# Two graph attention layers as one fixed-order pipeline over groups of edges, in a graph network on one core

## The chip, the core and the metric

The kernel runs on one core of a Trainium2 chip. A core has TensorE (PE in the profile; its weight loads are shown as PEld), VectorE (DVE), ScalarE (ACT), GpSimd (POOL) and SyncE (SP), which issues most transfers. The metric is the device time of one execution in microseconds, lower is better. All data are float32.

## The reference

A graph has 3125 nodes with 256 channels and 53125 edges, sorted by their destination node; each edge has 32 attributes and one of three types. Two attention layers run over the edges, then three relational layers:

```python
def transformer_conv(x, ...):             # 4 heads of 64 channels
    q, k, v = x @ wq + bq, x @ wk + bk, x @ wv + bv
    alpha = sum(q[dst] * k[src], -1) / sqrt(64)          # per edge and head
    ex = exp(alpha - segment_max(alpha, dst)[dst])
    alpha = ex / segment_sum(ex, dst)[dst]
    return segment_sum(v[src] * alpha, dst) + x @ ws + bs
h = leaky_relu(batch_norm(transformer_conv(x, layer 1)))
h = leaky_relu(batch_norm(transformer_conv(h, layer 2)))
x = layernorm(x + h)
# three times: message = relu(x[src] * (edge_attr @ nn_w.T + nn_b)),
# the mean of the messages per destination and type, @ W[type], summed, + x @ root + bias
out = layernorm(x + relational(x))
```

Batch norm goes over the nodes for each channel, layer norm over the channels of each node.

## The kernel before

The nodes lie in 25 blocks of 128, the edges in 416 tiles of 128 (the last ones padded); eight tiles make a group (G), and there are 52 groups (NG). A partition holds one node between the layers (tiles `xf` and `hf`, 128 x 25 x 256).

`gnn_kernel` builds tables of indices from `src`, `dst` and the types (L146 to L251): the source of each edge for the gathers, the position of its destination in a window of 32 nodes, a penalty where two neighbouring edges have different destinations, the first node of each pair of tiles. Shifted copies of the destinations go through a table in DRAM (`dp`). A flag says whether the edges have the expected form; the program branches on it to `sorted_edges` (L264), which is what runs here.

`window_attention` (L325) is called once for each layer. It has three stages.

1. The projection, for each block of 128 nodes: two transposes (L352), ScalarE's copy (L354), four matmuls of 128x512 for queries, skip, keys and values (L358), VectorE's adds of the biases (L362 to L369). Queries are stored to the table `qw_tab`, keys and values to `kvw_tab` with 4 x 65 columns for the values, whose 65th is 1.0 and later gives the denominator.
2. The loop over groups. `logits(g)`: GpSimd gathers eight times 128 rows of `kvw_tab` by source (L272, tile `kvg`, 4 buffers). SyncE loads the positions (`ldb`, L394), reads four row numbers into registers and loads four windows of 32 query rows (`qw`, L400). VectorE makes one-hot matrices (`oht`, L402), PE expands the queries to the edges with 32-row matmuls (`qdf`, L407), VectorE multiplies with the keys (`prod`, L409) and reduces per head (L411). `sums(g-1)`: SyncE loads the penalties (`pn`, L416); PE turns the logits (L420), VectorE finds the largest logit of each destination by a scan forward and one backward (L423, L425), PE turns it back (L428), VectorE subtracts (L431), ScalarE takes exp (L432). VectorE makes a one-hot over 32 nodes (L434) and multiplies it with the weights, for four heads, twice 128x512 (L438). PE sums weights times values in 32 matmuls with 32 columns of weights and 65 of values (L447), and VectorE adds the results into the accumulator (`accf`, L453, eight instructions with a column offset from registers). In layer 1 `attributes(g)` also turns the edge attributes for the later relational layers: a load of 1 KB per partition (L463), eight transposes (L468), two copies by ScalarE (L469), a store of whole rows to `at_d` (L470).
3. After the loop: a division by the denominators (L484 to L486), 16 transfers that bring the sums back to nodes on partitions (`naf`, L491), an add to the skip (L493), and `batch_norm` (L507 to L528), which sums over nodes with a matrix of ones on PE and applies the result on VectorE.

Behind layer 2 come the residual add (L300), `layer_norm` (L1252 to L1258), the store of `h_tab` (L303), the memset of the relational accumulator (`kacc`, L309) and `window_relational` (L563 to L660), which gathers rows of `h_tab` in the same groups of eight.

In the attention stages the order of instructions on each engine comes from the framework's scheduler, by the program's order and by buffers; only `window_relational` has an order written out by hand. SyncE issues its transfers one after another in its own order, and waits ahead of each for what that one reads.

Of the kernel before, what the change touches and what calls it, by code (L numbers as in the profile page):

```python
# [8 lines left out]
F32 = mybir.dt.float32  # L9
# [9 lines left out]
P = 128  # L19
# [33 lines left out]
W2 = 32  # L53
KN = 42
# [6 lines left out]
def last_group(i, rows):  # L61

    return min(NG - 1, int((E / N * rows * (i + 1) / P + SLACK) // G))

# [38 lines left out]
def gnn_kernel(ctx: ExitStack, tc: tile.TileContext, A, out):  # L103


    nc = tc.nc
# [5 lines left out]
    dp = dram.tile([FP + EP + 2 * P], F32, name="dp")  # L112
    pen_d = dram.tile([FP + EP + 2 * P], F32, name="pen_rows")
    ld_d = dram.tile([EP], F32, name="ld_rows")

    ident = const.tile([P, P], F32, name="identf")
    make_identity(nc, ident)
    src_c = const.tile([P, T], I32, name="src_c")
    lm_c = const.tile([P, T], F32, name="lm_c")
    kr_c = const.tile([P, T], F32, name="kr_c")  # L120
    a_off = const.tile([1, PR], I32, name="a_off")
    q_row = const.tile([1, PR], I32, name="q_row")
    k_off = const.tile([1, Q4], I32, name="k_off")
    a_low = const.tile([P, PR], F32, name="a_low")
    a_high = const.tile([P, PR], F32, name="a_high")
    k_low = const.tile([P, Q4], F32, name="k_low")
    k_high = const.tile([P, Q4], F32, name="k_high")
    flag = const.tile([1, 1], I32, name="flag")

    with tc.tile_pool(name="lk", bufs=1) as sp, tc.tile_pool(name="lkps", bufs=2, space=PSUM) as ps:  # L130
        rows = {}
        for name in ("dst", "src", "edge_type_3"):
# [4 lines left out]
            else:  # L137
# [7 lines left out]
        d = sp.tile([RB, B, P], F32, name="d_f")  # L145
        V.tensor_copy(d, rows["dst"])  # L146
        SY.dma_start(dp[FP:FP + EP].rearrange("(b r c) -> r b c", b=B, c=P), d)
        edge = sp.tile([1, FP + 2 * P], F32, name="edge")
        V.memset(edge[:, :FP], -1.0)
        GP.iota(edge[:, FP:].rearrange("o (a c) -> o a c", c=32), pattern=[[1, 8], [0, 32]], base=N + 4,  # L150
                channel_multiplier=0, allow_small_or_imprecise_dtypes=True)
        SY.dma_start(dp[:FP].unsqueeze(0), edge[:, :FP])
        SY.dma_start(dp[FP + EP:].unsqueeze(0), edge[:, FP:])

        prv = sp.tile([RB, B, P], F32, name="prv")
        nxt = sp.tile([RB, B, P], F32, name="nxt")
        SY.dma_start(prv, dp[FP - 1:FP - 1 + EP].rearrange("(b r c) -> r b c", b=B, c=P))
        SY.dma_start(nxt, dp[2 * FP:2 * FP + EP].rearrange("(b r c) -> r b c", b=B, c=P))
        n0 = sp.tile([RB, B], F32, name="n0")
        n4 = sp.tile([RB, B], F32, name="n4")  # L160
        for b in range(B):
            SY.dma_start(n0[:, b:b + 1], view(dp, FP + b * RB * P, [[2 * P, RB // 2], [0, 2], [1, 1]]))
            SY.dma_start(n4[:, b:b + 1], view(dp, FP + b * RB * P, [[4 * P, RB // 4], [0, 4], [1, 1]]))
        n0r = sp.tile([1, PR], F32, name="n0r")
        n4r = sp.tile([1, Q4], F32, name="n4r")
        SY.dma_start(n0r, view(dp, FP, [[0, 1], [2 * P, PR]]))
        SY.dma_start(n4r, view(dp, FP, [[0, 1], [4 * P, Q4]]))


        pen = sp.tile([RB, B, P], F32, name="pen")  # L170
        V.tensor_tensor(pen, d, prv, op=OP.is_equal)
        V.tensor_scalar(pen, pen, -1.0, BIG, op0=OP.add, op1=OP.mult)
        SY.dma_start(pen_d[FP:FP + EP].rearrange("(b r c) -> r b c", b=B, c=P), pen)
# [5 lines left out]

        ld = sp.tile([RB, B, P], F32, name="ld")  # L180
        V.tensor_tensor(ld, d, bc(n0, 2, P), op=OP.subtract)
        SY.dma_start(ld_d.rearrange("(b r c) -> r b c", b=B, c=P), ld)
        dq = d.rearrange("r b c -> r (b c)")
        _, dm = floor42(V, sp, dq, [RB, B * P], "d42")
# [5 lines left out]
        bad = sp.tile([RB, B, P], F32, name="bad")  # L190
        v = sp.tile([RB, B, P], F32, name="v")
        need = sp.tile([1, NG - 1], F32, name="need")
        V.memset(need, 0.0)
        for i in range(NT):
            V.memset(need[:, last_group(i, KM):], float((i + 1) * KM)) if last_group(i, KM) < NG - 1 else None
        V.tensor_tensor(need, need, n4r[:, 2::2], op=OP.subtract)
        late = sp.tile([1, 1], F32, name="late")
        V.tensor_reduce(late, need, AX.X, OP.max)
        V.tensor_tensor(bad, prv, d, op=OP.subtract)
        V.tensor_tensor(v, d, nxt, op=OP.subtract)  # L200
        V.scalar_tensor_tensor(bad, v, 1.0, bad, op0=OP.add, op1=OP.max)
        V.scalar_tensor_tensor(bad, ld, -float(W2 - 1), bad, op0=OP.add, op1=OP.max)
        V.tensor_tensor(v, d, bc(n4, 2, P), op=OP.subtract)
        V.scalar_tensor_tensor(bad, v, -float(KN - 1), bad, op0=OP.add, op1=OP.max)
        worst = sp.tile([RB, 1], F32, name="worst")
        V.tensor_reduce(worst, bad.rearrange("r b c -> r (b c)"), AX.X, OP.max)
        wt = ps.tile([1, RB], F32, name="wt")
        TE.transpose(wt, worst, ident[:RB, :RB])
        w1 = sp.tile([1, 1], F32, name="w1")
        V.tensor_reduce(w1, wt, AX.X, OP.max)  # L210
        V.tensor_tensor(w1, w1, late, op=OP.max)
        V.tensor_single_scalar(flag, w1, 0.0, op=OP.is_le)


# [5 lines left out]
        for col, v in ((src_c, s_f), (lm_c, lm), (kr_c, kr)):  # L220
            t = ps.tile([P, T], F32, name="colf")
            for b in range(B):
                TE.transpose(t[:, b * RB:(b + 1) * RB], v[:, b, :], ident[:RB, :RB])
# [1144 lines left out]
```

## Time and profile before

| what | value |
|---|---|
| median of 11 runs | 3477.54 us (3460.57 to 3483.32) |
| the profiled execution: time | 3480.43 us |
| its span, first to last instruction | 3478.6 us |
| mean granted clock of TensorE | 0.750 of full speed |
| busy PE / VectorE / ScalarE / GpSimd | 2591.2 / 2238.2 / 625.0 / 2129.8 us |
| first gather of layer 1, of layer 2, of the relational stage | 158.4, 1015.1, 1705.5 us from the start |

The profile is a page on one execution: busy time per engine, the span in 40 slices of 87 us with a digit in tenths for each engine, the chain of work that ended last, and groups of instructions by line, engine and tile, with their mean duration and what ended the idle time before them. The trace behind it also gives a timeline of single instructions and the busy times in any stretch. In a row such as `kvg<-kvw_tab,src_c` the tile written stands left of the arrow. PE, DVE, ACT, POOL and SP are the engines above; "issue" is time in which an engine waited for nothing that the profile shows; the granted clock is the share of full speed that the throttle gave TensorE.

### The profile page before, as it was taken

The page shows a single profiled execution, that of the slowest core. Times are in us where ns is not written, and L with a number is a line of the kernel's source. Part 1 is how long each engine was busy: PE and PEld are TensorE (multiplying, and loading weights), DVE is VectorE, ACT ScalarE, POOL GpSimd, SP SyncE. Part 2 cuts the span into 40 slices and gives each one's busy share as a digit, 9 for nine tenths or more (in the row PEclk, how much of TensorE's full clock was granted, in tenths as well). Part 3 has the DMA queues.
Part 4 walks back from the last instruction along what each step waited for, and adds up shares of the span by engine and source line. Part 5 has one row for each costly group of instructions (what it writes and reads, how often), then busy time and mean ns, then how long its engine had stood idle before and what let it go on. Part 6 is the DMA issues. An engine that isn't in the chain of part 4 may idle for free.

```text
span 3478.6 us, 49513 instructions
## 1 busy us (share of the span) xinstructions
PE 2591.2 (74%) x16663; PEld 1748.9 (50%) x16663; DVE 2238.2 (64%) x4344; ACT 625.0 (18%) x1060; POOL 2129.8 (61%) x2146
## 2 busy tenths in 40 slices
PE   4877777772886777773188888868888886888887
PEld 2444444542444444442166565646556654666665
DVE  4476767895548988894866665545555554666664
ACT  0122222000100000001022222212222221222222
POOL 0165655771027777760377777757777766777774
PEclk9955555555985555556599999978999988998888
DMA  4386766774148888873344444334343433444442
GB/s 125 125 238 198 218 202 197 228 228 109 49 141 234 232 229 232 233 207 70 117 119 116 120 116 118 109 96 116 115 116 113 116 97 101 122 119 122 120 127 77
DMA packets 296342, 510.28 MB, mean 147 GB/s; under 512 B 78243, under 2 KB 194833, under 8 KB 296081
## 3 DMA queue, kind: packets, MB, share of 16 engines
q0 software_dynamic: 126464, 383.52, 38.5%
q1 hardware_dynamic: 169617, 123.51, 11.9%
q8 instruction: 136, 2.23, 0.3%
q14 instruction: 125, 1.02, 0.1%
HBM read 459.91 MB, written 40.36 MB: 144 GB/s over the span
## 4 chain that ended last, share of the span: by engine, by line
PE 22%; POOL 19%; issue 11%; DVE 9%; DMA 7%; ACT 1%; SPq 1%; DVEq 0%; POOLq 0%; ACTq 0%
POOL xsf L272 18%; PE ppf L595 7%; DMA xsf<-h_tab,src_c 6%; PE qdf L407 5%; PE ewf L579 3%; PE of L447 3%; PE opf L642 2%; PE mtf L631 1%; DVE accf L453 1%; POOL kvg L272 1%; DVE xsf L586 1%; DVE kacc L608 1%; DVE mk L620 1%; PE alt L420 1%; DVE alf L411 1%
## 5 line engine op out<-in xcount | busy, mean ns | idle before, releaser
L272 POOL DMA_INDIRECT xsf<-h_tab,src_c x1248 | 1301.1, 1043 | 554.5 <-issue 345.7
L272 POOL DMA_INDIRECT kvg<-kvw_tab,src_c x832 | 820.1, 986 | 701.6 <-DMA qw_tab<-qs 341.6
L595 PE MATMUL ppf<-xsf,ohkf 128*126 128x256 f32 (+1 forms) x2496 | 709.7, 434 | 135.4 <-ACT xsf L587 53.1
L586 DVE TENSOR_TENSOR xsf<-xsf,ewf 128x1024 f32<-128x1024 f32 x312 | 380.4, 1219 | 617.7 <-DMA xsf<-h_tab,src_c 477.0
L595 PEld LDWEIGHTS ppf<-xsf,ohkf 128*126 128x126 f32 x2496 | 524.1, 219 | 261.1 <-ACT xsf L587 84.2
L407 PE MATMUL qdf<-qw,oht 32*128 32x256 f32 x1664 | 515.5, 659 | 16.4 <-DVE prod L409 8.0
L587 ACT ACTIVATE xsf<-xsf 128x1024 f32<-128x1024 f32 x312 | 329.9, 1057 | 947.0 <-DVE xsf L586 943.8
L579 PE MATMUL ewf<-nnwf,atw 33*128 33x256 f32 x2496 | 371.1, 418 | 0.9 <-ACT nnwf L320 0.9
L407 PEld LDWEIGHTS qdf<-qw,oht 32*128 32x128 f32 x1664 | 308.2, 311 | 124.3 <-DVE prod L409 24.6
L409 DVE TENSOR_TENSOR prod<-qdf,kvg 128x512 f32<-128x512 f32 x416 | 278.5, 681 | 40.7 <-PE qdf L407 22.0
L642 PE MATMUL opf<-rwt,mts 128*126 128x256 f32 x1200 | 301.3, 396 | 0.0
L579 PEld LDWEIGHTS ewf<-nnwf,atw 33*128 33x128 f32 x2496 | 226.8, 196 | 133.1 <-PE ppf L595 57.5
L411 DVE TENSOR_REDUCE alf<-prod 128x8 f32<-128x512 f32 x416 | 279.8, 674 | 0.1
L642 PEld LDWEIGHTS opf<-rwt,mts 128*126 128x126 f32 x1200 | 217.1, 190 | 73.0 <-issue 46.7
L447 PE MATMUL of<-kvg,ohw 128*32 128x65 f32 x6656 | 204.1, 315 | 47.9 <-DVE ohw L438 19.3
L631 PE MATMUL mtf<-identf,mk 126*128 126x126 f32 x450 | 97.7, 335 | 180.8 <-DVE mk L620 178.4
L447 PEld LDWEIGHTS of<-kvg,ohw 128*32 128x32 f32 x6656 | 180.3, 172 | 102.8 <-DVE ohw L438 31.5
L420 PE MATMUL alt<-identf,alf 128*32 128x128 f32 x312 | 102.8, 398 | 160.3 <-ACT fmax L424 134.3
L358 PE MATMUL pjf<-wf,xts 128*128 128x512 f32 x400 | 183.6, 615 | 13.8 <-ACT xts L354 5.7
L570 DVE TENSOR_TENSOR ohkf<-iotas,kr_c 128x1008 f32<-128x1008 f32 x156 | 187.5, 1202 | 0.0
L468 PE MATMUL atpf<-identf,ab 128*32 128x128 f32 x416 | 110.6, 403 | 86.4 <-ACT atr L469 46.3
L631 PEld LDWEIGHTS mtf<-identf,mk 126*128 126x128 f32 x450 | 55.6, 163 | 236.6 <-DVE mk L620 183.2
(159 smaller groups left out, 2062.6 us busy)
## 6 DMA issues: line engine op xcount, KB each, us to landing
atw<-at_d SPq DMA_DIRECT2D x312, 66.0 KB
xsf<-h_tab,src_c POOLq DMA_INDIRECT x1248
ldb<-ld_rows SPq DMA_DIRECT2D x104, 128.0 KB
kvg<-kvw_tab,src_c POOLq DMA_INDIRECT x832
qw<-qw_tab SPq DMA_DIRECT2D x416, 32.0 KB
kvw_tab<-kvs SPq DMA_DIRECT2D x50, 258.0 KB
at_d<-atr SPq DMA_DIRECT2D x52, 128.0 KB
ab<-in_edge_attr_dram SPq DMA_DIRECT2D x51, 128.0 KB
```

Source lines behind the costliest of these rows:

```text
L272: return GP.indirect_dma_start(out=dst, out_offset=None, in_=table, in_offset=rows_of(idx))
L407: TE.matmul(qd[:, k, :], oht[r, k, :], qw[r, :], start=True, stop=True)
L409: V.tensor_mul(pr, qd, kv[:, 2 * a:2 * a + 2, :D])
L411: V.tensor_reduce(al[:, t:t + 2, :], pr.rearrange("p t (h c) -> p t h c", h=H), AX.X, OP.add)
L447: TE.matmul(o[q * W2:(q + 1) * W2, a, :], ohw[:, j, q, :], kv[:, j, D + q * HC:D + (q + 1) * HC], start=(k == 0), stop=(k == 1))
L570: V.tensor_tensor(oh, bc(iota[:, :KM], 1, G), bc(L["kr_c"][:, g * G:(g + 1) * G], 2, KM), op=OP.is_equal)
L579: TE.matmul(ew[:, k, a, :], ats[g][r, 2 * u + a, :], nnw[r, :], start=True, stop=True)
L586: V.tensor_tensor(xk, xk, ews.pop(q), op=OP.mult)
L587: S.activation(x4, x4, AF.Relu)
L595: TE.matmul(pp[:, :wide], ohs[g][:, j, :], xss[g][:, j, :wide], start=(k == 0), stop=(k == 3))
L631: TE.transpose(t[:, b * KM:(b + 1) * KM], q["k"][:, b, c * P:(c + 1) * P], ident[:KM, :KM])
L642: TE.matmul(o, q["m"][:, c, r, :], w[:, r, c, :], start=(r + c == 0), stop=(r == R and c == 1))
```

## The change

The attention layers become one function with an order written out by hand for each engine (`tc.manual_schedule()`), and the channels lie on partitions between the layers (`xT`, 128 x 2 x 3200).

- Start: the shifted destinations are made with PE's transposes instead of the table in DRAM. `x` is loaded and turned to `xT`, and keys and values of layer 1 are projected in 13 pairs of blocks ahead of the branch, with one PSUM buffer, their adds behind the index work on VectorE.
- Loop: iteration `it` works on several groups at different stages: loads for it+3, gathers for it+2 (6 buffers), one-hots for it+1, logits for it, transposes for it-1, scans, exp and weights for it-2, one-hots over a whole block of 128 nodes for it-3, sums for it-4, the add for it-5. ScalarE multiplies the gathered values by their weights in place, 32 instructions of 128x65 a group with the weight as a scale per partition; PE sums with eight matmuls 128x128 by 128x260; VectorE adds twice instead of eight times. Products and reductions are taken four tiles at a time.
- Queries are projected inside the loop, every second iteration. When all edges of a block are through, it is divided, turned back and added to its skip projection by PE, and its statistics are taken by VectorE (`bn_stats`).
- The attributes of the edges are loaded in 1024 pieces of 128 bytes, turned in two transposes and one copy, and stored by four transfers.
- Between the layers batch norm is a scale and bias per partition on ScalarE and leaky relu on VectorE, pairwise, each pair followed by its projection to keys and values. Behind layer 2 the same steps, transposes to nodes on partitions, residual and layer norm run in seven rounds of four tiles.
- `window_relational` keeps its code.

The core of the diff, new code with a plus sign in the older functions:

```diff
@@ gnn_kernel @@
-        SY.dma_start(prv, dp[FP - 1:FP - 1 + EP].rearrange("(b r c) -> r b c", b=B, c=P))
...
+        for i in range(0, NT, 2):
+            n = min(2, NT - i)
+            for u in range(i, i + n):
+                tp = ps2.tile([P, T], F32, name="colf")
+                for k in range(2):
+                    TE.transpose(tp[:, k * P:(k + 1) * P], x[:, u, k * P:(k + 1) * P], ident)
+                S.copy(xT[:, :, u * P:(u + 1) * P], tp[:, :2 * P].rearrange("p (k c) -> p k c", k=2))
+            pj = ps.tile([P, 2, 2 * D], F32, name="pjf")
+            keys_values(tc, xT, i, n, w, pj)
+            st = wp.tile([P, 2, KV], F32, name="kvs")
...
@@ keys_values, store_keys_values: new @@
+def keys_values(tc, xT, i, n, w, pj):
+    for u in range(n):
+        for k in range(2):
+            tc.nc.tensor.matmul(pj[:, u, :], xT[:, k, (i + u) * P:(i + u + 1) * P], w[:, k, :],
+                                start=(k == 0), stop=(k == 1))
...
+def store_keys_values(tc, i, n, bias, pj, st, table):
+    V, SY = tc.nc.vector, tc.nc.sync
+    V.tensor_tensor(st[:, :n, :D], pj[:, :n, :D], bc(bias[:, :D], 1, n), op=OP.add)
+    for u in range(n):
+        v4 = st[:, u, D:].rearrange("p (h c) -> p h c", h=H)
+        V.tensor_tensor(v4[:, :, :HD], pj[:, u, D:].rearrange("p (h c) -> p h c", h=H),
+                        bias[:, D:].rearrange("p (h c) -> p h c", h=H), op=OP.add)
+    V.memset(st[:, :n, D:].rearrange("p t (h c) -> p t h c", h=H)[:, :, :, HD:], 1.0)
...
@@ window_attention: rewritten for both layers @@
-            for g in range(NG):
-                logits(g)
-                if g:
-                    sums(g - 1)
-                if n == 1:
-                    attributes(g)
...
+    with tc.tile_pool(name="a1", bufs=1) as one, tc.tile_pool(name="kvf", bufs=6) as kp, \
+            tc.tile_pool(name="a3", bufs=3) as sp, tc.tile_pool(name="a2", bufs=2) as sp2, \
+            tc.tile_pool(name="qdp", bufs=2, space=PSUM) as qps, \
+            tc.tile_pool(name="pop", bufs=2, space=PSUM) as pps, \
+            tc.tile_pool(name="a1p", bufs=1, space=PSUM) as ps1, tc.manual_schedule():
...
+        def loads(n, g):
+            ldb = sp.tile([P, 2 * P], F32, name="ldb")
+            SY.dma_start(ldb, view(L["ld_d"], g * G * P, [[2 * P, 4], [0, W2], [1, 2 * P]]))
+            qw = sp.tile([P, D], F32, name="qw")
+            _, at = nc.values_load_multi_w_load_instructions(
+                L["q_row"][:, g * 4:g * 4 + 4], engines=[SY.engine], min_val=0, max_val=N + 3,
+                skip_runtime_bounds_check_because="a pair's first dst: a node, or one of the padding's")
+            for a in range(4):
+                SY.dma_start(qw[a * W2:(a + 1) * W2, :], q_tab[bass.ds(at[a], W2), :])
+            lds[g], qws[g] = ldb, qw
...
+        def queries(g, u):
+            qd = qps.tile([P, 2, 2, D], F32, name="qdf")
+            for k in range(2):
+                for a in range(2):
+                    r = slice((2 * u + a) * W2, (2 * u + a + 1) * W2)
+                    TE.matmul(qd[:, a, k, :], ohts[g][r, k, :], qws[g][r, :], start=True, stop=True)
+            qds[g, u] = qd
+        def logits(g, u):
+            kv = kvs[g][:, 4 * u:4 * u + 4, :D]
+            V.tensor_mul(kv, qds.pop((g, u)).rearrange("p a k c -> p (a k) c"), kv)
+            t = g * G + 4 * u + 1
+            V.tensor_reduce(al[:, t:t + 4, :], kv.rearrange("p t (h c) -> p t h c", h=H), AX.X, OP.add)
+        def turn(g):
+            for s in range(3):
+                TE.transpose(alt_p[:, s, :], al[:, g * G + s:g * G + s + G, :].rearrange("p t h -> p (t h)"), ident)
...
+        def weigh(g):
+            TE.matmul(less_p, ident, al[:, g * G + 1:g * G + G + 1, :].rearrange("p t h -> p (t h)"),
+                      start=True, stop=False)
+            TE.matmul(less_p, fs.pop(g)[:, 64:64 + P], neg, start=False, stop=True)
+            w = sp2.tile([P, G * H], F32, name="wts")
+            S.activation(w, less_p, AF.Exp, scale=scale)
+            for j in range(G):
+                for q in range(H):
+                    c = kvs[g][:, j, D + q * HC:D + (q + 1) * HC]
+                    S.activation(c, c, AF.Copy, scale=w[:, j * H + q:j * H + q + 1])
...
+        def sums(g):
+            oh, kv = ohs.pop(g), kvs.pop(g)
+            po = pps.tile([P, AC], F32, name="pof")
+            for j in range(G):
+                TE.matmul(po, oh[:, j, :], kv[:, j, D:], start=(j == 0), stop=(j == G - 1))
+            pos[g] = po
...
+        def project_queries(i):
+            p = node[:, 1, :]
+            for k in range(2):
+                TE.matmul(p, xT[:, k, i * P:(i + 1) * P], wqs[:, k, :D], start=(k == 0), stop=(k == 1))
+            q = sp2.tile([P, D], F32, name="qs")
+            V.tensor_add(q, p, bq)
...
+            def skip():
+                p = node[:, 0, :].rearrange("p (k c) -> p k c", k=2)
+                for c in range(2):
+                    for k in range(2):
+                        TE.matmul(p[:, c, :], wqs[:, k, D + c * P:D + (c + 1) * P], xT[:, k, blk],
+                                  start=(k == 0), stop=False)
+                    TE.matmul(p[:, c, :], q["a"][:, c * P:(c + 1) * P], ident, start=False, stop=True)
+                for c in range(2):
...
+            ab = sp2.tile([P, G, DD], F32, name="ab")
+            lo, m = g * G * P, min(G, TF - g * G)
+            if m < G:
+                V.memset(ab, 0.0)
+                SY.dma_start(ab[:TR, m, :], A["edge_attr_32"][TF * P:, :])
+            SY.dma_start(ab[:, :m, :], A["edge_attr_32"][lo:lo + m * P, :].rearrange("(t e) d -> e t d", e=P))
+            p = node[:, 0, :].rearrange("p (k c) -> p k c", k=2)
+            for k in range(2):
+                TE.transpose(p[:, k, :], ab[:, 4 * k:4 * k + 4, :].rearrange("e t d -> e (t d)"), ident)
+            at = sp2.tile([P, 2, P], F32, name="atr")
+            S.copy(at, p)
+            for t in range(4):
+                SY.dma_start(view(L["at_d"], lo + t * P, [[EP, DD], [4 * P, 2], [1, P]]),
+                             at[t * DD:(t + 1) * DD])
...
+        def normalise(sc, a, b):
+            for c in range(2):
+                y = xT[:, c, a:b]
+                S.activation(y, y, AF.Identity, scale=sc[:, 0, c:c + 1], bias=sc[:, 1, c:c + 1])
+                V.scalar_tensor_tensor(y, y, 0.1, y, op0=OP.mult, op1=OP.max)
...
+            if n == 2:
+                w2, bias2 = kv_next
+                kv_tab = dram.tile([NP, KV], F32, name="kv_tab2")
+                for i in range(0, NT, 2):
+                    m = min(2, NT - i)
+                    normalise(sc, i * P, (i + m) * P)
+                    if i % 8 == 0:
+                        st = kp.tile([P, G, KV], F32, name="kvg")
+                    pj = qps.tile([P, 2, 2, D], F32, name="qdf").rearrange("p a k c -> p a (k c)")
+                    keys_values(tc, xT, i, m, w2, pj)
...
+            while it < NG + 5 or steps:
+                if it + 3 < NG:
+                    loads(n, it + 3)
+                if it + 1 < NG:
+                    penalties(it + 1)
+                    windows(it + 1)
+                if it < NG:
+                    queries(it, 1)
+                    logits(it, 0)
+                if 0 <= it - 4 < NG:
+                    sums(it - 4)
+                if 0 <= it - 2 < NG:
+                    maxima(it - 2)
+                    weigh(it - 2)
+                if it < NG:
+                    logits(it, 1)
+                if 0 <= it - 1 < NG:
+                    turn(it - 1)
+                if 0 <= it - 3 < NG:
+                    nodes_of(it - 3)
+                if 0 <= it - 5 < NG:
+                    add(it - 5)
+                if n == 1 and it < NG:
+                    attributes(it)
+                for s in steps[:2]:
+                    s()
+                steps = steps[2:]
+                while done < NT and it - 5 == last_group(done, P):
+                    steps += finish(done)
+                    done += 1
+                if it % 2 == 0 and i < NT:
+                    project_queries(i)
+                    i += 1
+                if it + 1 < NG:
+                    queries(it + 1, 0)
+                if it + 2 < NG:
+                    rows(it + 2, kv_tab)
...
+        for i in range(0, NT, 4):
+            m = min(4, NT - i)
+            normalise(sc, i * KM, (i + m) * KM)
+            t = qps.tile([P, 2, 2, D], F32, name="qdf").rearrange("p a k c -> p (a k) c")
+            for u in range(m):
+                for c in range(2):
+                    TE.transpose(t[:KM, u, c * P:(c + 1) * P], xT[:, c, (i + u) * KM:(i + u + 1) * KM], ident)
+            y = xrs[i // 16][:, i % 16:i % 16 + m, :]
+            V.tensor_tensor(y, y, t[:KM, :m, :], op=OP.add)
+            for u in range(m):
+                st = sp.tile([KM, 6], F32, name="lnst")
+                V.bn_stats(st, y[:, u, :])
+                V.bn_aggr(mv[:, i + u, :], st)
+            e = slice(i, i + m)
+            S.activation(rs[:, 0, e], mv[:, e, 1], AF.Sqrt, bias=L["eps"][:KM])
+            V.reciprocal(rs[:, 0, e], rs[:, 0, e])
+            V.scalar_tensor_tensor(rs[:, 1, e], mv[:, e, 0], -1.0, rs[:, 0, e], op0=OP.mult, op1=OP.mult)
+            for u in range(m):
+                S.activation(y[:, u, :], y[:, u, :], AF.Identity, scale=rs[:, 0, i + u:i + u + 1],
+                             bias=rs[:, 1, i + u:i + u + 1])

```

## The prediction

> **What bounds the kernel now.** I read the 40 slices first, to cut the span into stages:
>
> ```profile
> PE   4877777772886777773188888868888886888887
> ...
> DVE  4476767895548988894866665545555554666664
> ...
> POOL 0165655771027777760377777757777766777774
> PEclk9955555555985555556599999978999988998888
> ```
>
> A slice is 87 us. GpSimd (POOL), which gathers the source rows, works in slices 3 to 9, 13 to 18 and from 21 on; between them lie the start and two gaps. The timeline sets the edges: index work to 34, projection 46 to 146, first gather 158.4, first product of logits 165.9, layer 1 to 827.4, the second layer's first product 1021.5, layer 2 to 1582.7, first relational gather 1705.5. The 1773 us from there are relational and unchanged, so the change plays within 1705. Per group (52 a layer) layer 1 takes 661.5/52 = 12.7, layer 2 561/52 = 10.8.
>
> Then the table by stretch (length; busy time of PE, PEld, DVE, ACT, POOL; granted clock; DMA share; GB/s):
>
> ```profile
> 200.00:300.00 100.00, 72.79 (x683) 42.56 (x681) 68.24 (x165) 22.87 (x36) 61.23 (x63) 0.52 0.75 221
> ...
> 860.00:950.00 90.00, 64.88 (x197) 38.65 (x198) 49.97 (x71) 16.13 (x39) 0.00 (x0) 0.85 0.17 58
> ...
> 1150.00:1300.00 150.00, 111.41 (x1213) 71.91 (x1216) 134.21 (x328) 6.26 (x29) 115.09 (x115) 0.51 0.80 229
> 1590.00:1720.00 130.00, 24.95 (x100) 20.34 (x100) 74.28 (x102) 12.65 (x29) 11.29 (x13) 0.61 0.31 84
> 1720.00:2300.00 580.00, 470.03 (x2283) 341.59 (x2284) 343.25 (x491) 143.52 (x207) 432.86 (x464) 0.91 0.40 115
> ```
>
> In layer 2 VectorE is 89% busy and POOL 77%, but POOL's busy share leaves out what the timeline shows between two gathers:
>
> ```profile
> 1015.11 0.94 POOL L272 DMA_INDIRECT kvg<-kvw_tab,src_c  x1 [218.04 <-DMA qw_tab<-qs]
> 1016.36 0.94 POOL L272 DMA_INDIRECT kvg<-kvw_tab,src_c  x1 [0.30 <-issue]
> ```
>
> One gather every 1.25 us; with the page's mean of 986 ns, eight take 8 x 1.286 = 10.3. Layer 2 (10.8) stands almost on that floor, which the change keeps; layer 1 has 2.4 to give, and the start and the gaps more.
>
> **The change, part by part**
>
> **Start.** 13 pairs of blocks are projected ahead of the flag, with one PSUM buffer, so that each pair takes its four matmuls of 128x512 (4 x 0.89 = 3.56 us, L358 at full clock), three adds and a memset (1.45, by 128x512 at 0.68) and a handover (0.2): 5.2. The adds stand on VectorE behind the index work (34 before, some 3 more with transposes in place of the shifted rows through DRAM): 37 + 13 x 5.2 = 104. Skip weights 4, acc memset 5.5, four query projections 10, table landing 2.3 and window 2 lie partly in a row: first product at 124 instead of 165.9, a gain of **42**. Bounds 110 to 140.
>
> **Layer-1 loop.** What goes: 28 of 32 small sums' overhead on PE, and VectorE's one-hot products (two of 0.687). What comes, per group: ScalarE weights 32 slices of 128x65 by a column. No row has that form; the nearest:
>
> ```profile
> L354 ACT COPY xts<-xtf 128x256 f32<-128x256 f32 x50 | 16.6, 375 | 190.3 <-PE xtf L352 163.0 <-PE pjf L358 27.3
> ...
> L656 ACT ACTIVATE rsr<-mvr,epss 126x1 f32<-126x1 f32 x25 | 7.4, 294 | 84.9 <-DVE mvr L654 84.9
> L521 ACT ACTIVATE scf<-sumsqf,epss 128x256 f32<-128x256 f32 x2 | 0.9, 473 | 0.0
> ```
>
> Between 294 (one column) and 473 (256), 65 columns are about 340 ns alone. Two copies back to back took 0.65 for 2 x 0.372, so neighbours overlap by 0.09: I take 0.25, 32 x 0.25 = 8.0, with exp 0.23 and a copy or skip 8.5. Upper end 32 x 0.34 + 0.6 = 11.5; lower end, if only the 65 columns counted (179/255 x 65 = 46 ns), below 3.5. The Trainium skill, "ScalarE: Activation LUTs", section "Rules for kernel authors", would have a multiplication on VectorE; its section "What ACT_TABLE_LOAD costs" gives, as an estimate, (186 + 54 + 93 - 93) ns x 32 = 7.7 us, which agrees with my 8.0 and leaves ScalarE below POOL's floor, so here the rule would cost nothing by itself.
>
> POOL's floor is 10.3; VectorE has two products and two reductions of 128x1024 (5.0 by L409 and L411), one-hots 1.2 + 0.4, scans 1.25, adds 1.0, rest 0.6: 9.4. Neither binds layer 1. What does is a loop through SyncE's fixed order. In each iteration SyncE issues, in a row: the stores of the turned attributes, which wait for ScalarE's copy, then ldb, the register load, four query windows, penalties, and only then the load of the next attributes, whose transposes stand in PE's order ahead of all else. That is S, from copy to transposes done: stores 4 x 0.4 = 1.6, ldb 0.6, register load 0.5, windows 1.9, penalties 0.8, attribute load 1.0, its landing 3.0 (bounds 1.3 to 4.3, the rows of before's attribute load and of its small-piece transfers), two transposes 0.55, and every second time a wait for the query table (0.7): **10.7**. After the transposes PE does Q until the next group's exp can start: queries 2.28 (L579, four in 1.14 at full clock), sums 8 x 0.48 = 3.85 (L595, four 128x257 in 1.9), mask 0.4, half of skip 1.5 and project 1.0, waits 0.4: **8.2**. Then ScalarE does A = **8.5** and the next copy but one. So two periods are S + Q + A = 27.4, one 13.7: **712 for 52 groups**, where before spent 661.5. Every store now also stands ahead of a load, so a slower landing shows at half its price. Bounds by the ends of A and landing: 10.7 to 15.5. The tail (iterations 52 to 56 with the last blocks) I put at 34.
>
> **Gap 1.** Divide, 16 transfers, batch norm by matmuls go from 827-1015; in their place statistics 5, then 13 pairs (12.5 x 6.0: ScalarE 0.95, VectorE 0.96 for leaky relu, PE 3.56, adds partly beside) and 24 to the first product: **104**, where before had 1021.5 - 827.4 = 194. The pairs go in a row, as VectorE's next leaky relu stands behind the adds that wait for PE.
>
> **Layer 2.** No attributes: nothing ties ScalarE to SyncE. POOL 10.3, VectorE 9.4, ScalarE 8.5, PE 8.6 at full clock; I take 10.7: **556**, tail 34. PE's skip waits for VectorE's divide, and the next queries stand behind it; PE's slack of 1.7 covers that, and without the cover 1 in 25 blocks costs 25.
>
> **Gap 2.** 1582.7 to 1700.1 (117) becomes seven rounds of about 10 in a row (normalise 2, eight transposes 2.5, add and statistics 3, root and scale 2.5): **71**.
>
> **Sum**: 124 + 712 + 34 + 104 + 556 + 34 + 71 = 1635 against 1700: 65 less. On the profiled execution (span 3478.6, time 3480.4) that is a span of 3414 and a time of 3415; this execution lay 2.9 over the median 3477.5, so **3413**.
>
> **Clock.** Before, PE in attention was granted 0.51 to 0.52, in the relational stage, with full-width matmuls, 0.91. There a slack stretch is followed by a slow one (3.4 us each):
>
> ```profile
> 2013.60:2017.00 3.40, 1.31 (x10) 0.87 (x10) 3.03 (x7) 1.06 (x1) 2.48 (x4) 0.94 0.72 211
> 2017.00:2020.40 3.40, 3.40 (x12) 2.85 (x11) 1.99 (x3) 0.69 (x3) 2.49 (x4) 0.56 0.43 124
> 2020.40:2023.80 3.40, 3.19 (x20) 2.18 (x19) 2.54 (x4) 1.65 (x3) 2.92 (x4) 1.00 0.25 77
> ```
>
> I price Q warm because the new sums use all 128 rows and PE is busy 60 to 80%; cold, sums take 6.1 (four 128x257 in 3.04), queries 4.1 (L407, four in 2.07), the rest 1.8: Q = 12. The Trainium skill, "TensorE: Matmul & The Clock Gate", Part 1, "What's actually happening", says that one idle window of about 3.4 us halves the clock until a busy one has passed. The rows show such a drop after a stretch 39% busy, thus not idle, and speak more against the change than the rule does: in layer 1 the wait for the attributes leaves PE such a gap in each group.
>
> **The rivals**
>
> - **B, the loop does not bind.** If the landing takes 1.3 and activations 0.1, S + Q + A is under 20.6 and POOL rules: P = 10.7 and 10.5, 156 + 10 us less, and with fuller overlap in start and gaps (the bounds above, 60) about 3190 to 3250. I use **3247**. For it: POOL has done 10.0. Against: SyncE's order.
> - **C, slower: PE at half clock.** Q = 12 gives P1 = (10.7 + 12 + 8.5)/2 = 15.6 and, with PE then the bound at 12.2, P2 = 12.2: 99 + 78 = 177 over the forecast, **3590**; in layer 1 alone with 0.3 in layer 2, 3526. Place: PE's wait for the attributes' DMA. Break-even: the loops and tails may cost 65/52 = 1.25 more in P1 + P2 than my 24.4; from 25.6 on it is slower. For it: 0.52 now. Against: 0.91 in the relational stage at the same POOL rhythm.
> - **E, ScalarE's activations stand one behind another.** 32 x 0.34: A = 11.5, P1 = 15.2, P2 = 12: 78 + 68, **3559**.
> - **Does it do what it says?** That the fixed order does not hold is excluded: the order of each engine is written out in the program.
>
> **How the numbers follow.** Forecast A .45 (own range 3360 to 3470), B .20, C .25, E .10. 0.2% (7 us) is about what a measurement of this kernel can tell from no change. Faster: .39 of A and B's .20 = .59; the same: .04 of A and .01 of C = .05; slower: .02 + .24 + .10 = .36. The range 3255 to 3585 leaves out the lower half of B and the upper fifth of C and E's edge, some .17.
>
> **What would show it.** Right: in layer 1, SyncE's stores wait for ScalarE's copy and PE's transposes for the attribute load, period 13 to 14; in layer 2 gathers 1.25 apart with gaps under 1 per group, period 10.7; first product near 124; ScalarE busy 625 + 104 x 8 - some 90 of old copies = 1360 us; clock over 0.8. Wrong: a clock of 0.5 in either loop (C), activations over 0.3 each in a row (E), POOL without idle time in layer 1 (B), or VectorE over 95% busy, which I cost at nothing: its 9.4 hides under POOL's 10.3, and 1 more would cost 52 a layer.

## The result

The changed kernel takes 3593.84 us (median of 8, 3585.1 to 3603.94), the kernel before 3476.35 (31 runs): **3.4% slower**, ratio 1.0343 [1.0328, 1.0358]. The forecast was 3413, faster. The profiled execution took 3601.88, with a span of 3600.1, 121.5 over that of before. Some of the experiments ran where every kernel took 12 to 17% longer, the kernel before 4020 to 4080 us, though a gather still took 0.95 us; they stand in the lower half of the table of runs, and their times are compared only with each other.

The slices of the changed kernel, the lines shown of before:

```profile
PE   5356655666666777777358888868888886878887
...
DVE  4255555556536678778456555545655554666665
ACT  1055554455623677768412222212222221222222
POOL 0534544455206767765087777757777775777774
PEclk9667766777786788878679888888989998999988
```

GpSimd starts one slice earlier, but works at 3 to 5 tenths through layer 1, where before it had 5 to 7; PE mostly at 5 and 6. In layer 2 (slices 13 to 18) it is back at 6 and 7. So the loss lies in layer 1, not in ScalarE's or PE's total. In the costliest groups, the rows that the estimate turned on:

```profile
L365 POOL DMA_INDIRECT kvg<-kv_tab,src_c x832 | 831.0, 999 | 740.6 <-ACT wts L489 349.6
...
L493 ACT ACTIVATE kvg<-kvg,wts 128x65 f32<-128x65 f32 x3328 | 808.7, 335 | 3.8 <-ACT wts L489 0.3
```

An activation lasts 335 ns, but 3328 of them fill 808.7: they overlap, and cost 0.243 each. Stage by stage, in us (loops per group; "rest" from the first relational gather on). In the forecast and in the changed kernel a loop runs to the last reduction of logits, and what is still on its way then counts to the gap; in the kernel before it runs to the last add. By the last reduction its loops take 12.4 and 10.5:

| | first product | layer 1 | gap 1 | layer 2 | gap 2 | rest |
|---|---|---|---|---|---|---|
| before | 165.9 | 12.7 | 194 | 10.8 | 123 | 1773 |
| forecast | 124 | 13.7 | 138 | 10.7 | 110 | 1773 |
| changed | 143.7 | 15.8 | 154.5 | 11.1 | 106 | 1798 |

Of the 186 us by which the profiled span exceeds the forecast's 3414, layer 1 has (821 - 712) = 109, the rest 25, layer 2 and the start 20 each, gap 1 16; gap 2 gives 4 back.

**What ends last in layer 1.** The chain of waits of the changed kernel through one group (start, length, what):

```profile
559.26 1.22 PE nodeps L543 x4
560.48 0.43 PE nodeps L545 x2
560.91 0.85 PE nodeps L543 x4
561.76 0.43 PE nodeps L545 x2
562.19 1.93 PE qdf L461 x16
564.12 3.70 PE pof L504 x16
567.83 0.14 PE soft L485 x2
567.97 0.39 PE soft L487 x2
568.36 0.02 issue
568.38 0.21 ACT wts L489
568.59 0.02 issue
568.61 4.96 ACT kvg L493 x21
...
573.65 2.73 ACT kvg L493 x11
576.38 0.26 ACT atr L568
576.65 0.04 issue
576.69 2.07 PE nodeps L521 x4
```

PE and ScalarE work in turns: skip, queries, sums, mask on PE (9.1), exp and 32 scalings on ScalarE (8.0), then ScalarE's copy of the turned attributes (`atr`, L568), and only then may PE begin again. The transposes and PE's next matmuls (skip L543, query projection L521) use one PSUM tile, `nodeps`, and wait until the copy has read it, also where they write its other half (L521). One group costs 9.1 + 8.0 + 0.3 = 17.4 here. PE's waits in layer 1 from 204 us on, so without its first groups (us in all, times, longest):

```profile
PE nodeps L566 <- DMA ab<-in_edge_attr_dram: 181.5, 48, 10.2
PE nodeps L543 <- ACT atr L568: 53.4, 21, 5.8
PE nodeps L521 <- ACT atr L568: 40.1, 11, 5.2
```

The largest wait by this list is that for the attributes' load, which was the forecast's; the chain names the copy. Which one would give time back, only a run can tell.

### The profile page after: what moved, and what is told of

Read it like the earlier page. It is cut to its first block, busy times and chain, and to the rows that moved or that the text cites. A ratio compares the mean times of both kernels' runs of the same rounds, so it can differ in the third digit from the quotient of the medians.

```text
span 3600.1 us, 41458 instructions
## 1 busy us (share of the span) xinstructions
PE 2563.0 (71%) x12104; PEld 1848.1 (51%) x12104; DVE 2087.2 (58%) x3185; ACT 1355.2 (38%) x4327; POOL 2165.0 (60%) x2145
## 3 DMA queue, kind: packets, MB, share of 16 engines
q1 hardware_dynamic: 205107, 118.69, 11.5%
## 4 chain that ended last, share of the span: by engine, by line
PE 31%; POOL 19%; DVE 13%; ACT 12%; issue 12%; DMA 11%; SPq 1%; DVEq 0%; ACTq 0%; POOLq 0%
POOL xsf L365 18%; ACT kvg L493 10%; PE ppf L775 6%; PE pof L504 6%; DMA xsf<-h_tab,src_c 5%; PE qdf L461 3%; PE ewf L759 3%; DMA ab<-in_edge_attr_dram 2%; PE opf L822 2%; DVE kvg L466 2%; DMA kvg<-kv_tab,src_c 2%; PE nodeps L521 2%; PE qdf L340 2%; PE nodeps L543 2%; PE pjf L340 1%
## 5 line engine op out<-in xcount | busy, mean ns | idle before, releaser
L365 POOL DMA_INDIRECT xsf<-h_tab,src_c x1248 | 1325.7, 1062 | 431.3 <-issue 348.4
L365 POOL DMA_INDIRECT kvg<-kv_tab,src_c x832 | 831.0, 999 | 740.6 <-ACT wts L489 349.6
L493 ACT ACTIVATE kvg<-kvg,wts 128x65 f32<-128x65 f32 x3328 | 808.7, 335 | 3.8 <-ACT wts L489 0.3
L504 PE MATMUL pof<-kvg,ohn 128*128 128x260 f32 x1664 | 450.6, 429 | 40.7 <-DVE accf L515 37.7
L504 PEld LDWEIGHTS pof<-kvg,ohn 128*128 128x128 f32 x1664 | 347.2, 215 | 154.9 <-DVE accf L515 48.4
L466 DVE TENSOR_TENSOR kvg<-qdf,kvg 128x1024 f32<-128x1024 f32 x208 | 250.8, 1206 | 234.7 <-PE qdf L461 225.8
L468 DVE TENSOR_REDUCE alf<-kvg 128x16 f32<-128x1024 f32 x208 | 253.8, 1220 | 7.2
L461 PE MATMUL qdf<-qw,oht 32*128 32x256 f32 x1664 | 189.9, 571 | 20.4 <-DVE oht L452 10.6
L566 PE MATMUL nodeps<-identf,ab 128*128 128x128 f32 x104 | 33.3, 420 | 216.1 <-DMA ab<-in_edge_attr_dram 210.5
L813 ACT COPY mts<-mtf 128x378 f32<-128x378 f32 x150 | 71.1, 474 | 278.4 <-PE mtf L812 276.6
```

The lines of the kernel that those rows point to most:

```text
L365: return GP.indirect_dma_start(out=dst, out_offset=None, in_=table, in_offset=rows_of(idx))
L461: TE.matmul(qd[:, a, k, :], ohts[g][r, k, :], qws[g][r, :], start=True, stop=True)
L466: V.tensor_mul(kv, qds.pop((g, u)).rearrange("p a k c -> p (a k) c"), kv)
L468: V.tensor_reduce(al[:, t:t + 4, :], kv.rearrange("p t (h c) -> p t h c", h=H), AX.X, OP.add)
L493: S.activation(c, c, AF.Copy, scale=w[:, j * H + q:j * H + q + 1])
L504: TE.matmul(po, oh[:, j, :], kv[:, j, D:], start=(j == 0), stop=(j == G - 1))
```

## The experiments

Two theories on layer 1 are told apart. T1: PE waits for the copy behind the scalings, through the PSUM tile. T2, the forecast's: SyncE's row and the landing bind. Layers are in us a group.

| run | layer 1 | layer 2 | us | ratio to before |
|---|---|---|---|---|
| **kernel before at 3476 to 3479** | | | | |
| changed | 15.8 | 11.1 | 3593.8 | 1.0343 [1.0328, 1.0358] |
| g1, early load | 14.4 | 11.1 | 3531.5 | 1.0153 [1.0131, 1.0175] |
| g5, own PSUM tile as well | 11.2 | 10.8 | 3356.3 | 0.9650 [0.9624, 0.9675] |
| e8, memset in parts | 15.8 | 11.1 | 3586.4 | 1.0316 [1.0293, 1.0338] |
| e9, copy first and more | 11.4 | 11.0 | 3363.2 | 0.9679 [0.9661, 0.9696] |
| **kernel before at 4020 to 4080** | | | | |
| c1, changed | 16.5 | 13.3 | 4023.4 | 0.9998 [0.9965, 1.0030] |
| e1 / f1, early load | 16.3 / 16.0 | 13.5 / 13.3 | 4029.8 / 3981.1 | 0.9868 [0.9810, 0.9927] / 0.9915 [0.9884, 0.9947] |
| e2 / f2, copy first | 13.9 / 13.7 | 13.4 / 13.4 | 3907.4 / 3876.2 | 0.9560 [0.9522, 0.9598] / 0.9639 [0.9596, 0.9682] |
| e5 / f5, own tile | 13.8 / 13.7 | 13.3 / 13.5 | 3873.3 / 3887.9 | 0.9632 [0.9581, 0.9683] / 0.9676 [0.9630, 0.9722] |
| e3, division early | 16.6 | 13.6 | 4079.7 | 0.9983 [0.9960, 1.0007] |
| e4 / f4, two tiles on VectorE | 15.4 / 15.5 | 13.3 / 13.7 | 3999.9 / 3976.7 | 0.9802 [0.9763, 0.9841] / 0.9893 [0.9851, 0.9935] |
| e6, late load | 16.9 | 13.4 | 4025.6 | 1.0025 [0.9999, 1.0050] |
| e7, e2 + e3 + e4 + e6 | 13.3 | 13.1 | 3835.1 | 0.9555 [0.9513, 0.9597] |
| e10, e5 + e3 + e4 + e8 | 14.1 | 13.4 | 3879.8 | 0.9677 [0.9613, 0.9742] |

**e1, f1, g1: the attributes loaded one iteration ahead.**

```diff
+                if n == 1 and it + 1 < NG:
+                    fetch(it + 1)           # memset and load only
                 if n == 1 and it < NG:
                     attributes(it)          # transposes, copy, stores
```

> Only change: in layer 1 the attributes of the next group are loaded one iteration ahead of their transposes, ahead of the stores. Layer 1 of the changed kernel took 821 us from the first product to the end of the last (15.8 a group); PE waited 181 us for this load and 94 us for ScalarE's copy. Theory T1 (the copy of the turned attributes stands on ScalarE behind 32 scalings, and PE's next matmuls write the same PSUM tile and wait for it, so that one group costs PE's row of 8.5 plus ScalarE's 8.4): the wait moves from the load to the copy, layer 1 stays at 15.5 to 17 a group, time within -20 to +60 of the changed kernel's 3594. Theory T2 (the prediction's: SyncE's row and the landing are the term to cut): layer 1 falls by 2 to 3.5 a group, time 3410 to 3490.

> The kernel of e1 again, on a chip where the kernel before takes about 3477 us. T1: layer 1 between 15.5 and 17 a group (changed kernel 15.8), ratio to the kernel before 1.03 to 1.05. T2: 12.3 to 13.8 a group, ratio 0.98 to 1.00.

> The kernel of e1 at the speed of the prediction, if this chip has it (kernel before about 3477 us). T1: layer 1 between 15.3 and 17 a group (changed kernel 15.8), ratio 1.02 to 1.05. T2: 12.3 to 13.8 a group, ratio 0.98 to 1.00.

In the lower half of the table layer 1 lost at most 0.5 a group, as T1 says. In the upper half it fell from 15.8 to 14.4, between the two expectations. PE's waits in g1's layer 1, again from 204 us on:

```profile
PE nodeps L543 <- ACT atr L572: 154.2, 21, 7.3
PE nodeps L521 <- ACT atr L572: 80.8, 11, 7.3
```

The wait for the load is gone, and that for the copy has grown from 94 to 235. The distance from one group's first product to the next tells why both theories hold in part. In groups 20 to 36 it is 17.1 on average, in the changed kernel and in g1 alike. Three such products of the changed kernel (start, length):

```profile
564.18 1.23 DVE L466 TENSOR_TENSOR kvg<-qdf,kvg 128x1024 f32<-128x1024 f32 x1 [8.28 <-PE qdf L461]
...
580.82 1.23 DVE L466 TENSOR_TENSOR kvg<-qdf,kvg 128x1024 f32<-128x1024 f32 x1 [1.27 <-PE qdf L461]
...
598.34 1.23 DVE L466 TENSOR_TENSOR kvg<-qdf,kvg 128x1024 f32<-128x1024 f32 x1 [8.13 <-PE qdf L461]
```

There skip and query projection fall into alternate iterations, so that PE needs the tile back in every one. In the other stretches both fall into the same iteration, and a long group takes turns with a short one: mostly 17 to 24 with 9 to 12 in the changed kernel (15.2 on average, without the first distance of 25.4), 18.4 with 8.7 in g1 (13.2). Three of g1's:

```profile
262.47 1.22 DVE L466 TENSOR_TENSOR kvg<-qdf,kvg 128x1024 f32<-128x1024 f32 x1 [0.36 <-PE qdf L461]
...
271.15 1.22 DVE L466 TENSOR_TENSOR kvg<-qdf,kvg 128x1024 f32<-128x1024 f32 x1
...
289.56 1.23 DVE L466 TENSOR_TENSOR kvg<-qdf,kvg 128x1024 f32<-128x1024 f32 x1 [0.36 <-PE qdf L461]
```

Only there was the landing in the loop.

**e5, f5, g5: a PSUM tile of their own for the attributes**, the copy still behind the scalings; the add moves to the start of the iteration, because the sums have one buffer left.

```diff
-            tc.tile_pool(name="pop", bufs=2, space=PSUM) as pps, \
+            tc.tile_pool(name="pop", bufs=1, space=PSUM) as pps, \
...
-            p = node[:, 0, :].rearrange("p (k c) -> p k c", k=2)
+            p = pps.tile([P, 2, P], F32, name="atp")
```

> As e1 (attributes loaded one iteration ahead), and their transposes write a PSUM tile of their own, made free by a single buffer for the sums, for which the add into the accumulator moves to the start of the iteration. ScalarE's copy stands behind the 32 scalings as in the changed kernel. T1 (PE waits for this copy because the next matmuls write the same tile): PE's waits for the copy (58 + 103 us in e1's layer 1) go, layer 1 comes within 0.7 a group of layer 2, 120 to 230 less than the changed kernel on this chip. If the copy's place on ScalarE costs by itself, through SyncE's stores or the query table, layer 1 stays within 0.5 a group of e1 and the time within 30 of the changed kernel.

> The kernel of e5 again. T1: 11.1 to 12 a group in layer 1 though the copy stands behind the scalings, ratio 0.965 to 0.98. If the copy's place costs by itself: within 0.5 a group of f1.

> The kernel of e5 at the speed of the prediction, if this chip has it. T1: 11.1 to 12 a group in layer 1, ratio 0.965 to 0.98. If the copy's place on ScalarE costs by itself: within 0.5 a group of g1.

As T1 says: 14.4 to 11.2 a group against g1, and the kernel is faster than the kernel before. What PE waits for longest in g5's layer 1, from 204 us on:

```profile
PE nodeps L545 <- DVE naf L537: 39.4, 21, 3.5
PE pof L504 <- DVE accf L515: 35.7, 24, 2.3
PE nodeps L521 <- ACT xT L547: 33.1, 8, 5.5
```

No copy of attributes is left in it. Both kinds of stretch have become shorter: groups 20 to 36 take 10.5, the others 11.4. Some 0.2 of the 3.2 may belong to the moved add, as layer 2 gained that much too.

**e2, f2: transposes and copy ahead of exp and scalings**, with e1's early load.

```diff
+                    attributes(it)
                 if 0 <= it - 2 < NG:
                     maxima(it - 2)
                     weigh(it - 2)
...
-                    attributes(it)
```

> As e1, and the transposes and the copy of the attributes also stand ahead of the exp and the scalings of that iteration on PE and ScalarE. T1: the loop through ScalarE is cut, layer 1 falls to layer 2's 11.1 to 12 a group: 4.0 to 4.7 x 52 = 210 to 245 less, time 3350 to 3385, below the kernel before (3476). T2: the same as e1, as the landing is hidden in both: a difference between e1 and e2 of under 30. Rival T3 (TensorE's clock: 0.70 in layer 1): no more than 2 a group comes back, time above 3490.

> The kernel of e2 again. T1: 11.3 to 12 a group in layer 1, ratio 0.967 to 0.98. T2: as f1.

2.3 to 2.4 less than e1 and f1, down to 0.3 to 0.5 above layer 2: the order alone does what the tile does.

**e4, f4: VectorE weights two of the eight tiles.**

```diff
-            for j in range(G):
+            for j in range(6):
...
+            V.tensor_tensor(v, v, bc(w, 3, HC), op=OP.mult)     # tiles 6 and 7, behind nodes_of
```

> Only change: of the eight tiles of a group VectorE weights two with one multiplication, ScalarE six (24 instead of 32 activations, 2.0 us less a group). T1, one group in the loop: layer 1 falls by 2.0 x 52 = 104; T2, two groups in the loop: by 1.0 x 52 = 52. Layer 2, where VectorE gets 0.6 a group more, within -10 to +20. Time 3480 to 3510 by T1, 3530 to 3560 by T2. If ScalarE were in no loop, no gain: 3590 to 3610.

> The kernel of e4 again. One group in the loop (T1): layer 1 from 15.8 to 13.8; two groups in the loop (T2): to 14.8. Ratio 1.00 to 1.005 by T1, 1.015 to 1.02 by T2.

Here T1 and T2 stand for one and for two groups in the loop. Layer 1 takes 1.0 to 1.1 a group less than c1 and e4 1.2 less than e3: nearer to two groups over the whole layer, so that one group in the loop throughout falls. By stretches both slopes are there: between groups 20 and 36 the distances go from 16.7 and 17.6 in c1 to 14.7 and 16.1 in f4, 1.8 less on average; elsewhere, without the first distance, the mean goes from 15.4 to 14.7. That middle stretch of c1 (17.1 on average) is also as long as in the changed kernel's first profile.

**e3: the division one iteration earlier.**

```diff
-                    steps += finish(done)
+                    divide, skip, stat = finish(done)
+                    divide()
+                    steps += [skip, stat]
```

> Only change: the division of a finished block is issued one iteration ahead of the skip projection that reads it. In layer 2 of the changed kernel PE waited 68 us for it (21 times) and a pair of groups took 22.2 where the gathers alone take 20.6. If this wait is what lies between 11.1 and the gathers' 10.3, layer 2 falls by 0.4 to 0.8 a group, 20 to 40 us in all, and layer 1, where other waits end later, by under 10: time 3550 to 3580. If it is covered (the prediction's figure for it was nothing), time within 8 of 3594.

No gain that can be told while layer 2 took 13.6, so this does not settle what the wait costs at 11.1. In e9 below, where the wait is gone and two tiles have moved to VectorE, layer 2 took 11.0.

**e6: the large load behind the first gathers**, and **e8: the memset in four parts**, both about the 25 us of the rest.

```diff
-        SY.dma_start(h, h_tab.rearrange("(i p) c -> p i c", p=KM))      # e6
...
+                SY.dma_start(h, first.rearrange("(i p) c -> p i c", p=KM))      # behind rows(n, 0, table)
...
-        V.memset(acc.rearrange("p k c -> p (k c)"), 0.0)                # e8
+        for a in range(0, size, 5000):
+            V.memset(flat[:, a:min(a + 5000, size)], 0.0)
```

> Only change: the load of the 3150 KB of node rows for the relational stage is issued behind that stage's first eight gathers. In the changed kernel and in all four experiments the first gather behind that load took 21.25 us, where one takes 0.95; 3150 KB in 20 us are 158 GB/s, about what the transfers move elsewhere. If the gather waits for that load, it falls to about 1 and 12 to 20 us go from the time. If it is VectorE's memset of 16.55 us beside it, the gather stays over 15 us and the time within 6 of the changed kernel.

> Only change: VectorE's memset of the relational accumulator (16.55 us) is cut into four of 3.9 to 4.2. In every run of the new order so far the first relational gather took 21.25 us, whichever chip and wherever the large load stood, and ended 1.87 to 1.89 after this memset. If the gather waits for VectorE while such an instruction runs, it ends after one of the first parts, at 8 to 13 us, and 8 to 13 us go from the time (of a ratio with the interval of these runs, hardly to be told). If it waits for something else, it stays at 21.25.

The gather and the memset in the changed kernel, from the timelines of GpSimd and of VectorE (start, length):

```profile
1801.73 21.25 POOL L365 DMA_INDIRECT xsf<-h_tab,src_c  x1 [0.55 <-issue]
1823.29 0.95 POOL L365 DMA_INDIRECT xsf<-h_tab,src_c  x1 [0.30 <-issue]
```

```profile
1804.56 16.55 DVE L383 MEMSET kacc<- 126x19789 f32 x1 [6.71 <-issue]
1821.02 1.15 DVE L750 TENSOR_TENSOR ohkf<-iotas,kr_c 128x1008 f32<-128x1008 f32 x1
```

With the load moved the gather stayed at 21.26. With the memset in parts the first gather took 0.95 and a later one 6.25, at the last part (4.05 us). GpSimd, then VectorE, in e8:

```profile
1819.87 0.95 POOL L365 DMA_INDIRECT xsf<-h_tab,src_c  x1 [0.30 <-issue]
1821.12 6.25 POOL L365 DMA_INDIRECT xsf<-h_tab,src_c  x1 [0.30 <-issue]
```

```profile
1821.45 4.05 DVE L386 MEMSET kacc<- 126x4789 f32 x1 [0.95 <-issue]
1825.41 1.14 DVE L753 TENSOR_TENSOR ohkf<-iotas,kr_c 128x1008 f32<-128x1008 f32 x1
```

So it is VectorE, not the load: the rest fell from 1798 to 1776, the time by 7 (intervals 1.0328 to 1.0358 and 1.0293 to 1.0338 still touch). That it is the memset itself is not shown. In all 18 profiles of the new order the long gather ended 0.81 to 0.82 after the end of `ohkf`, the comparison of two SBUF tiles that stands directly behind the memset. Gathers beside the first three parts, behind which another memset stands, took 0.95, and so did those beside the whole memset in the kernel before, behind which a product with an input in PSUM stands. And of the 241 gathers over 1.1 us in the changed kernel, 240 ended 0.7 to 0.9 after a VectorE instruction with both inputs in SBUF (`ohkf`, `ohn`, `mk` or `fmax`); of the 1839 shorter ones 60 did. By these rows the gather waits for `ohkf`, which itself waits behind the memset; no run moves `ohkf`, so this stays argued. The Trainium skill, "SBUF — State Buffer", section "SBUF: two separate sides", says that VectorE with two SBUF inputs and a GpSimd operation that reads SBUF share a pair of ports, which the one that starts first holds for its whole instruction. The ends of the gathers agree; that a gather which began 19.3 us before `ohkf` was held does not, and stays open.

**c0, c1: the kernels themselves.**

> The kernel before itself, for its profile on the chip on which the others run. On a chip where it takes 4000 us and more (two chips did so), the prediction's rows say that the gathers' issue does not change (0.95 + 0.30 us in the experiments too), so the time should have gone into waits for gathered rows, in both attention loops and in the relational stage (13.1 us a group in the changed kernel there, 11.3 on the first chip). On a chip where it takes 3477 us, the stages of the first profile.

> The changed kernel itself, as the measure for the others on this chip: the first four runs came from a chip on which the kernel before took 4080 us and stages that they did not touch were some 15 to 20% longer. Expected ratio to the kernel before 1.03 on a chip where that takes 3477 us, and about 1.00 on one where it takes 4080 us.

c0 took 3477.7, ratio 0.9999 [0.9989, 1.0010], with the stages of the first profile. So there is no profile of the kernel before at 4020 us, and why the change costs nothing there (c1: 0.9998) stays open.

**e7, e9, e10: edits together.**

> The edits of e2 (copy ahead of the scalings), e3 (division early), e4 (two tiles weighted by VectorE) and e6 (late load) together. T1: 2.7 x 52 = 140 (e2 against e3 on the first chip) to 230 (the prediction's floor) from e2, 10 to 25 from e4 in layer 2, 10 to 20 from e6, 0 to 15 from e3: 160 to 290 less than the changed kernel, faster than the kernel before.

> e2, e3, e4 together with the memset in four parts. On a chip where the kernel before takes about 4020 us: the ratio of the run with the late load, 0.956, within 0.005. On a chip where it takes 3477 us: layer 1 falls from 15.8 to 11.3 a group (234 less), layer 2 from 11.1 to 10.6 (26 less), 10 from the memset: about 3594 - 270 = 3325, ratio 0.955 to 0.965.

> e5 (own PSUM tile, early load, add first) with e3 (division early), e4 (two tiles weighted by VectorE) and e8 (memset in parts). In e5 at full gather speed layer 1 took 11.2 and layer 2 10.8 a group, with PE waits of 40 us for the division and 33 us for ScalarE's skip activations in layer 1, where the gathers' floor is 10.3. If these waits bind, both layers come to 10.4 to 10.7 and 8 us go from the memset: ratio to the kernel before 0.948 to 0.958 at full speed. If VectorE (9.4 and 0.6 more) binds instead, no gain over e5: 0.960 to 0.967.

e7 is not told from e2 alone (0.9555 and 0.9560), nor e10 from e5. e9 is 230 below the changed kernel; the 3325 expected was missed, with layer 2 at 11.0 instead of 10.6. The lowest time is g5's: 3356 us, 3.5% under the kernel before, not told from e9 by the intervals.

## Why the prediction was wrong

- **Layer 1, the step that failed**: "After the transposes PE does Q until the next group's exp can start." PE does not start after the transposes: its next matmuls wait for ScalarE's copy of their output, and that copy stands behind the scalings. I put the copy at the end of A, as something that only SyncE's stores wait for. So Q and A lie in a row in every group where skip and projection alternate: 9.1 + 8.3 = 17.4 instead of 13.7. Of the 109 us over the forecast, 55 lie in these 16 groups and 49 in the other stretches, where SyncE's row and the landing are in the loop as forecast, but a pair took 2 x 15.2 = 30 instead of 27.4; which term this 3 belongs to is not known. With a tile of its own for the copy's input (g5) both excesses go.
- Its terms were nearly right. An activation costs 0.243 (0.25 taken), Q's instructions 9.1 with a skip and 8.4 with a projection (8.2 on average taken; the skip alone 2.9, 1.5 taken), the landing 2.3 in the median (3.0). By its own ends of A and landing the upper bound of a period is (12.0 + 8.2 + 11.5) / 2 = 15.9, not 15.5; that the measured 15.8 lies below it is luck, as neither term was at its end. Two of the signs named for "right" came true as well, ScalarE busy 1355 us (1360) and a mean clock of 0.82: neither tells the forecast from a loop tied by the copy.
- **Rival C** named nearly the measured time (3590) by luck, not its cause: no loop ran at half clock. The granted clock in layer 1 was 0.72, and PE's busy time per group 463.5 us / (760 / 15.8) = 9.6 against g5's 385.0 / (520 / 11.2) = 8.3 at 0.86: by this the clock is worth 1.3 of the 4.6 at the most, and it went up when the wait went. In the chain above, where the groups are longest, the sums took 3.70, less than the 3.85 taken for full clock.
- **Rival E** is refuted by the 0.243. **Rival B** comes true in g5: with the loop cut, layer 1 is at 11.2 and layer 2 at 10.8, near B's 10.7 and 10.5. Its condition was wrong: not a shorter landing. By its own terms S + Q + A comes to 9.0 + 8.2 + 3.7 = 20.9 there, not under 20.6.
- **Start**: 143.7 instead of 124. Half of the 20 stands ahead of the loop's own loads: the index work on VectorE ended at 43.6 instead of 37 and a pair took 5.3 to 5.6 instead of 5.2, so that the last adds ended at 113.6 instead of 104. The other half is "table landing 2.3 and window 2", which took 14.6 from the last query bias on. A load issued at 129.50 was waited for until 138.80, while GpSimd's gathers ran; that they hold it up is not shown:

```profile
138.80 0.35 DVE L452 TENSOR_SCALAR oht<-ldb,wid 128x256 f32<-128x256 f32 x1 [9.71 <-DMA ldb<-ld_rows]
```

- **Gap 1**: a pair took 6.8 instead of 6.0. VectorE waited for PE's four matmuls 5.2 to 5.6 in two of the three pairs shown, at a granted clock of 0.63 and 0.69 while they ran, and 3.5 in the third, at 1.00:

```profile
1012.43 0.69 DVE L347 TENSOR_TENSOR kvg<-qdf,bkv 128x512 f32<-128x512 f32 x1 [5.64 <-PE qdf L340]
...
1019.81 0.69 DVE L347 TENSOR_TENSOR kvg<-qdf,bkv 128x512 f32<-128x512 f32 x1 [5.22 <-PE qdf L340]
...
1025.49 0.69 DVE L347 TENSOR_TENSOR kvg<-qdf,bkv 128x512 f32<-128x512 f32 x1 [3.52 <-PE qdf L340]
```

- **Layer 2**: 11.1 instead of 10.7. PE waited 68 us for the division, which I cost at nothing, and 35 for the add; with the add moved (g5) it is 10.8. What the division is worth by itself is not settled; in e9, without its wait but with two tiles more on VectorE, layer 2 is at 11.0.
- **Gap 2** was right (seven rounds of 10.3). **The rest** was costed at no change: 25 us, 20 of them through one gather held while VectorE had a memset, which both kernels have, and `ohkf` behind it.

## What to carry to other kernels

In an order written by hand, look at each buffer with one copy: who reads it last, and what stands ahead of that reader on its engine. A cheap copy (0.35 us) behind a long row of another stage (7.8) ties two engines into turns, though PE is busy for 61% and ScalarE for 54% of that stage. And the largest wait of a list need not be the one that gives time back: taking away 181 us of waiting for the load gave 62, as most of it turned into the next wait.

## What was not expected of the hardware

- One gather of 0.95 us took 21.25 us in fifteen profiles alike, though the 16.55 us memset on VectorE had begun 2.8 after it. It ended 0.82 after the comparison of two SBUF tiles that stands behind this memset, and 240 of the changed kernel's 241 gathers over 1.1 us ended just so, 0.7 to 0.9 after a VectorE instruction with two inputs in SBUF.
- Back-to-back activations of 128x65 with a scale per partition last 335 ns and start every 243.
